# Adaptive-norm transformer block: set-up with shift and scale from products on all partitions, h of the second batch among the rotations, turns between the runs, and means times powers by GpSimd

## The chip, the cores and the metric

The kernel runs on 1 core of one Trainium2 chip. The metric is the device time of the whole program in microseconds (us). TensorE (PE) multiplies matrices, VectorE (DVE) works elementwise and reduces, ScalarE (ACT) applies functions and scaled copies, GpSimd (POOL) works elementwise on SBUF, SyncE (SP) issues DMAs. DMAs are issued from the queues of SP, ScalarE and GpSimd.

## The reference

Everything is float32. x is 16 batches of 1024 rows by 256 columns; c is 16 x 256; wmod is 256 x 1536; there are 16 heads of 16 columns.

```python
mod = (silu(c) @ wmod).reshape(16, 6, 1, 256)
sa, ca, ga, sb, cb, gb = (mod[:, i] for i in range(6))
ga = sign(ga) * max(|ga|, 0.25)            # gb the same; sign(0) = 1
h = layernorm(x) * (1 + ca) + sa
x = x + ga * attention_block(h)            # h + Wo(softmax(rope(q) rope(k)^T / 4, causal) v) + bo,
                                           # q, k, v from layernorm(h) * ln_gamma + ln_beta
h = layernorm(x) * (1 + cb) + sb
x = x + gb * ffn(h)                        # 8 experts of 512 gathered rows each, scatter-add
```

So each batch needs two normalizations in a row ("x" and "h" in the names of the code): the first is scaled and shifted by that batch's rows of the modulation, and the second one's result is turned (transposed) for the products q, k and v. The modulation itself comes first of all: it is a product of all of c with wmod.

## The kernel before

The rows of a batch are two halves of 512 rows, a half four tiles of 128. The heads go in four groups of 4 (`G`). For each batch and group a pass of ten steps goes over the blocks of the causal triangle; steps 1 and 5 are *pair steps*, which take two narrow blocks at once (256 and 128 columns). A step does, for 4 heads: the scores of its block (L682, tile `s`), exp on ScalarE (L695, tile `p`), a select on GpSimd on diagonal blocks (L700), and the products with the values (L729, tile `o`), one step later. At the same time it works out the row maxima of the next pass: a product (L605, tile `m`) and a reduction on VectorE (L623, or L627 with the mask). Scores and maxima are issued in two bursts of four products, called runs in the title: `burst(0)`, then one other product (`first`), then `burst(1)`, then the `second`. All of these use six PSUM slots (`ps_s`, tag `s`), so a burst can begin only when the reductions and exps of products before it have freed slots.

Other work of the batch ahead is placed into these steps by hand: the turns (`step_xT`, L485, evacuated by ScalarE at L486 into `xnT`), q and k (`step_qk`, L510) with the rotations on VectorE (L517, tile `rot`) and their sums on GpSimd (`step_rot`, L533 and L534), written to DRAM and read back by head (`operands`), v (`step_v`, L541), the output projection (L821). `pieces` are TensorE's pieces, `extra` comes after a step, and `inside` is popped by VectorE one item after each reduction of a step (`between`), the rest by `drain()`.

`steps_h(b, half)` makes the two normalizations of one half: statistics (L387, L392) on VectorE, the power -0.5 on GpSimd (L397, L398, tile `rstd`), minus mean times power on VectorE (`less_mean`, L406, tile `nmr`), the normalization on ScalarE (L415), scale and shift with the rows of the modulation (`turn`, L428, on GpSimd; on VectorE for the first half of batch 0), and then for the residual `rest` (L438: bias bo and gate) and `onto` (L442). `H_AT` says at which group and step each of these stands for batches 2 and up. For batch 1 `spread` places them, and for batch 0 they are issued in the set-up.

The set-up, before the loop: loads; `modulation(half)`, which multiplies (L259), copies (L266), adds 1 and bounds the gates on 16 partitions (L268 to L275) and writes the result to DRAM (`mod_a` for the first half), from where `load_mod(b)` reads the three rows of a batch onto all partitions; the tables of the angles (`tables`, L290 to L297); batch 0's normalizations, turns, q, k and rotations; the maxima of the first pass (`own(n)`, ten units); v; batch 1's first half; `indices()`, which loads the experts' indices (L313) and transposes them (L318).

In the attention's end, `finish(c)` copies the sums of half c, sends the denominators through DRAM, takes the reciprocal on VectorE (L789, waits for the DMA `den`) and sends it back as `rec`; later GpSimd multiplies (L797). `to_do` puts the reciprocal inside step +2 and the multiplication after step +5 (half 0) or +4 (half 1):

```python
            inside[step + 2].append(first)
            extra[step + (4 if c else 5)].extend(others)
```

The order on TensorE, VectorE, ScalarE and GpSimd is that of the program; in the set-up that of SP too. What is computed after the attention (the experts) is not touched.

Of the kernel before, what the change touches and what calls it, by code (L numbers as in the profile page):

```python
# [19 lines left out]
P = 128  # L20
# [7 lines left out]
def adaln_block_kernel(  # L28
# [50 lines left out]
    mhalf = const.tile([P, NT], F32, name="mhalf")  # L79
    nc.vector.memset(mhalf, -0.5)  # L80
# [115 lines left out]
    with ExitStack() as actx:  # L196
# [54 lines left out]
        def modulation(half):  # L251
# [3 lines left out]
            m3 = mod[:B, o : o + 3 * D]  # L255
            for n in range(2):
                ps = ps_s.tile([P, QC], F32, name=f"pmod{half}_{n}", tag="s")
                for k in range(KC):
                    nc.tensor.matmul(  # L259
                        ps[:B, :w],  # L260
                        lhsT=sg[:, k, :],
                        rhs=wm[k][:, o + n * w : o + (n + 1) * w],
                        start=(k == 0),
                        stop=(k == KC - 1),
                    )
                nc.scalar.copy(m3[:, n * w : (n + 1) * w], ps[:B, :w])  # L266
# [32 lines left out]
        def output_bias():  # L299

            pbo = ps_1.tile([P, D], F32, name="pbo", tag="misc")
# [8 lines left out]
            nc.vector.tensor_tensor(bo_bc, pbo, bo_bc, ALU.add)  # L310

        def indices():
            nc.sync.dma_start(out=idx, in_=top_idx.rearrange("(t p) e -> p t e", p=P))  # L313
# [22 lines left out]
        def constants():  # L336
# [21 lines left out]
            for t in v_tiles:  # L358
                nc.gpsimd.memset(t, 0.0)
                nc.vector.memset(t[:, :, 0 : H * VW + 1 : VW], 1.0)  # L360
            for t in rec:
                nc.gpsimd.memset(t, 0.0)
            nc.vector.tensor_reduce(
# [11 lines left out]
        def steps_h(b, half, named=False):  # L375
# [5 lines left out]
            passes = nc.vector if (b, half) == (0, 0) else nc.gpsimd  # L381

            def stat(of, i):
                if i == 0:
                    mine["st"] = wk.tile([P, TC, 6], F32, name=f"st_{of}_{b}_{half}", tag="st")
                src = s["x"][:, half * TC + i, :] if of == "x" else s["h", half][:, i, :]
# [8 lines left out]
            def power(of):  # L395
                mine["r"] = wk.tile([P, TC], F32, name=f"rstd_{of}_{b}_{half}", tag="rstd")
                nc.gpsimd.tensor_tensor(mine["r"], mine["mv"][:, :, 1], eps[:, :TC], ALU.add)  # L397
                nc.gpsimd.tensor_tensor(mine["r"], mine["r"], mhalf[:, :TC], ALU.pow)  # L398

# [4 lines left out]
            def less_mean(of):  # L404
                mine["n"] = wk.tile([P, TC], F32, name=f"nmr_{of}_{b}_{half}", tag="nmr")
                nc.vector.scalar_tensor_tensor(mine["n"], mine["mean"], -1.0, mine["r"], ALU.mult, ALU.mult)  # L406

            def norm(of, u):
                if of == "x" and u == 0:
                    s["h", half] = lk.tile([P, TC, D], F32, name=f"h_{b}_{half}", tag="h")  # L410
                if u == 0 and not named:
                    less_mean(of)
                h = s["h", half]
                for i in (2 * u, 2 * u + 1):
                    nc.scalar.activation(  # L415
                        h[:, i, :],
                        s["x"][:, half * TC + i, :] if of == "x" else h[:, i, :],
# [8 lines left out]
            def turn(u, n, op):  # L426
                h = s["h", half][:, ts(u, 2), :]
                passes.tensor_tensor(h, h, row(n), op)  # L428

            def rest(u, n, op):  # L430
                if n is None and u == 0 and b > 0:
                    mine["rest"] = lk.tile([P, TC, D], F32, name=f"r_{b}_{half}", tag="r", bufs=1)
                elif n is None and u == 0:
                    if half == 0:
                        s["rest"] = big_tile([P, NT, D], "r_0")
                    mine["rest"] = s["rest"][:, ts(half, TC), :]
                r = mine["rest"][:, ts(u, 2), :]
                (passes if n is None else nc.gpsimd).tensor_tensor(r, s["h", half][:, ts(u, 2), :] if n is None else r, row(n), op)  # L438
# [5 lines left out]
            if named:  # L444
                pieces = {f"{of}{i}": lambda of=of, i=i: stat(of, i) for of in "xh" for i in range(TC)}
                for of in "xh":
                    pieces[of + " moments"] = lambda of=of: moments(of)
                    pieces[of + " power"] = lambda of=of: power(of)
                    pieces[of + " less"] = lambda of=of: less_mean(of)
                for u in range(2):  # L450
                    pieces[f"x norm{u}"] = lambda u=u: norm("x", u)
                    pieces[f"scale{u}"] = lambda u=u: turn(u, 1, ALU.mult)
                    pieces[f"shift{u}"] = lambda u=u: turn(u, 0, ALU.add)
                    pieces[f"bias{u}"] = lambda u=u: rest(u, None, ALU.add)
                    pieces[f"h norm{u}"] = lambda u=u: norm("h", u)
                    pieces[f"gate{u}"] = lambda u=u: rest(u, 2, ALU.mult)
                    pieces[f"onto{u}"] = lambda u=u: onto(u)
                return pieces

            return (  # L460
                [("v", lambda i=i: stat("x", i)) for i in range(TC)]
                + [("g", lambda: whole("x"))]
                + [("v", lambda u=u: norm("x", u)) for u in range(2)]
                + [("g", lambda u=u: turn(u, 1, ALU.mult)) for u in range(2)]
                + [("g", lambda u=u: turn(u, 0, ALU.add)) for u in range(2)]
                + [("v", lambda i=i: stat("h", i)) for i in range(TC)]
                + [("g", lambda: whole("h"))]
                + [("g", lambda u=u: rest(u, None, ALU.add)) for u in range(2)]
                + [("v", lambda u=u: norm("h", u)) for u in range(2)]
                + [("g", lambda u=u: rest(u, 2, ALU.mult)) for u in range(2)]  # L470
                + [("g", lambda u=u: onto(u)) for u in range(2)]
            )
# [388 lines left out]


        def spread(items, first, last):

            n = 0
            for at in range(first, last):
                want = -(-len(items) * (at - first + 1) // (last - first - 3))
                count = {"v": 0, "g": 0}
# [503 lines left out]
```

## Time and profile before

| what | before |
|---|---|
| runs | 2884.34, 2889.95, 2890.49 us, median 2889.95 |
| profiled execution | 2886.74 us, its span 2885.0 us |
| busy, share of the span: PE, DVE, ACT, POOL | 97%, 74%, 57%, 54% |
| first rotation (L517) | at 45.74 us |
| first reduction of the maxima (L627) | at 62.17 us |
| first scores (L682) | at 99.12 us |
| mean granted TensorE clock | 0.986 |

The page gives times from the start of the span. A row of the timeline has the start, the length, engine, line, operation and tiles, then in brackets the idle time of that engine before it and what ended it. A busy TensorE is not TensorE at its peak: matmuls overlap and their ends are modelled, so a stall inside a burst shows only in where the next matmul starts.

### The profile page before, as it was taken

Reading aid. Unit: us, or ns where it says so; the run is one execution under the profiler, and the core shown is the slowest. Engines: PE = TensorE matmul, PEld = TensorE weight load, DVE = VectorE, ACT = ScalarE, POOL = GpSimd, SP = SyncE. Lnnn points to the kernel's source line nnn. Section 1 sums busy time; section 2 is a strip of 40 time slices with the busy share of each in tenths; the row PEclk is TensorE's granted clock in tenths of the full one; section 3 lists DMA queues with packets and bytes.
Section 4 is the critical chain, followed back from the end, with each engine's and each line's share of the span. In section 5 each row is a group of like instructions: output and inputs, shape, how many; then the busy total and the mean of one; then the engine's idle time right before and its main releaser. Section 6 shows DMA issues by size and latency. Waiting matters only on the chain.

```text
span 2885.0 us, 62886 instructions
## 1 busy us (share of the span) xinstructions
PE 2810.8 (97%) x22373; PEld 1289.4 (45%) x22373; DVE 2125.2 (74%) x6810; ACT 1651.1 (57%) x3342; POOL 1562.6 (54%) x2063
## 2 busy tenths in 40 slices
PE   5899999999999999999999999999999999997998
PEld 3444444444444444444444444444444444443665
DVE  5777878777787878787877878787878777763554
ACT  2356666666666566666666666656666655653111
POOL 5455464546555555546454655555464666354553
PEclk7899999999999999999999999999999999998999
DMA  4211121222222222212222222222121212134552
GB/s 122 58 44 35 50 71 52 64 56 68 59 56 56 64 61 63 60 51 66 63 59 62 64 54 58 60 67 62 50 71 51 75 41 65 32 95 153 176 184 67
DMA packets 200154, 199.58 MB, mean 69 GB/s; under 512 B 93344, under 2 KB 154208, under 8 KB 199840
## 3 DMA queue, kind: packets, MB, share of 16 engines
q1 hardware_dynamic: 172240, 147.69, 18.9%
q0 software_dynamic: 8448, 24.78, 2.7%
q10 hardware_dynamic: 19152, 23.08, 2.6%
q8 instruction: 177, 2.90, 0.4%
q14 instruction: 137, 1.12, 0.1%
HBM read 118.67 MB, written 75.66 MB: 67 GB/s over the span
## 4 chain that ended last, share of the span: by engine, by line
PE 90%; DMA 3%; DVE 2%; POOL 2%; issue 1%; ACT 1%; SPq 0%; POOLq 0%; DVEq 0%; ACTq 0%
PE s L682 39%; PE o L729 20%; PE pqk L510 9%; PE m L605 7%; PE pw L821 4%; PE pv L541 4%; PE fo L1229 2%; PE ph L1204 2%; PE ptx L485 1%; DMA out_dram<-fy,idx 1%; DMA cur<-out_dram,idx 1%; POOL modg L98 1%; ACT p L695 0%; DMA ops<-rot 0%; DVE nmr_h L406 0%
## 5 line engine op out<-in xcount | busy, mean ns | idle before, releaser
L695 ACT ACTIVATE p<-s 128x512 f32<-128x512 f32 (+1 forms) x2560 | 1278.9, 552 | 895.5 <-PE m L605 797.4
L605 PE MATMUL m<-ko,qo 32*128 32x512 f32 (+3 forms) x6144 | 1439.5, 527 | 7.0 <-DVE mt L623 4.7
L682 PE MATMUL s<-qo,ko 32*128 32x512 f32 (+3 forms) x6144 | 1359.1, 526 | 0.6 <-DMA qo<-max 0.5
L700 POOL TENSOR_SCALAR_AFFINE_SELECT p<-p 128x256 f32<-128x256 f32 x1024 | 416.1, 414 | 1002.4 <-ACT p L695 1001.2
L623 DVE TENSOR_REDUCE mt<-m 128x1 f32<-128x512 f32 x1024 | 673.0, 683 | 203.9 <-PE m L605 184.2
L682 PEld LDWEIGHTS s<-qo,ko 32*128 32x128 f32 x6144 | 514.8, 183 | 597.3 <-issue 423.6
L729 PE MATMUL o<-p,v_pad 128*32 128x512 f32 (+3 forms) x6840 | 652.7, 464 | 3.2 <-POOL p L700 2.8
L627 DVE CUSTOM_DVE_ANT_0 masked<-m,dmask,mt 128x256 f32<-128x256 f32 (+3 forms) x1024 | 511.4, 539 | 142.6 <-PE m L605 132.1
L627 DVE CUSTOM_DVE_ANT_0 masked<-m,dmask 128x512 f32<-128x512 f32 (+3 forms) x1024 | 453.9, 485 | 189.3 <-PE m L605 170.2
L605 PEld LDWEIGHTS m<-ko,qo 32*128 32x128 f32 x6144 | 576.6, 184 | 30.2 <-DVE mt L627 11.2
L729 PEld LDWEIGHTS o<-p,v_pad 128*32 128x32 f32 x6840 | 149.0, 108 | 427.8 <-issue 180.0
L510 PE MATMUL pqk<-xnT,wqk 128*128 128x256 f32 x1024 | 287.3, 405 | 1.8 <-ACT xnT L486 1.3
L510 PEld LDWEIGHTS pqk<-xnT,wqk 128*128 128x128 f32 x1024 | 175.3, 190 | 193.0 <-issue 148.5
L428 POOL TENSOR_TENSOR h<-h,mod 128x512 f32<-128x512 f32 x124 | 157.6, 1274 | 76.5 <-ACT h L415 70.9
L627 DVE DVE_READ_ACCUMULATOR2_ANT mt<- 128x1 f32 x2048 | 168.7, 82 | 0.0
L541 PE MATMUL pv<-wv_sb,xnT 128*128 128x256 f32 x512 | 146.9, 410 | 1.1 <-ACT xnT L486 0.9
L821 PE MATMUL pw<-wo,onT 128*128 128x256 f32 x512 | 144.2, 405 | 0.6 <-DVE onT L778 0.6
L1207 ACT ACTIVATE gT<-ph,b_sb 128x512 f32<-128x512 f32 x64 | 44.0, 687 | 174.1 <-PE ph L1204 169.1
L541 PEld LDWEIGHTS pv<-wv_sb,xnT 128*128 128x128 f32 x512 | 87.9, 191 | 98.5 <-issue 76.5
L517 DVE SCALAR_TENSOR_TENSOR rot<-pqk,bcol,cosT 128x256 f32<-128x256 f32 x256 | 122.0, 477 | 11.6 <-PE pqk L510 8.3
L821 PEld LDWEIGHTS pw<-wo,onT 128*128 128x128 f32 x512 | 86.9, 189 | 89.3 <-issue 70.9
L517 DVE SCALAR_TENSOR_TENSOR rot<-pqk,bcol,sinT 128x256 f32<-128x256 f32 x256 | 121.3, 474 | 0.6 <-DMA ops<-rot 0.6
(122 smaller groups left out, 2239.5 us busy)
## 6 DMA issues: line engine op xcount, KB each, us to landing
ops<-rot SPq DMA_DIRECT2D x128, 256.0 KB
rec<-rec_d SPq DMA_DIRECT2D x504, 32.0 KB
rows<-y SPq DMA_DIRECT2D x62, 256.0 KB
out_dram<-y SPq DMA_DIRECT2D x62, 256.0 KB
w<-in_W_dram SPq DMA_DIRECT2D x14, 1024.0 KB
qo<-ops SPq DMA_DIRECT2D x192, 64.0 KB
ko<-ops SPq DMA_DIRECT2D x192, 64.0 KB
x<-in_x_dram ACTq DMA_DIRECT2D x24, 512.0 KB
```

The costliest lines, as they stand in the source:

```text
L428: passes.tensor_tensor(h, h, row(n), op)
L510: nc.tensor.matmul(ps, lhsT=wqk[:, k, n, e, :], rhs=xt[:, k, ts(u, QW)], start=(k == 0), stop=(k == KC - 1))
L517: nc.vector.scalar_tensor_tensor(s["rot", half, n, e, f][:, ts(u, QW)], ps, bcol[:, n, e : e + 1], tab[:, half * QC + u * QW : half * QC + ...
L541: nc.tensor.matmul(pv, lhsT=S[b]["xnT", t // TC][:, k, ts(t % TC, P)], rhs=wv_sb[:, k, :], start=(k == 0), stop=(k == KC - 1),)
L605: nc.tensor.matmul(sc[:, sum(w[:n]) : sum(w[: n + 1])], lhsT=q[rows, ts(i, P)], rhs=k[rows, c * QC : c * QC + w[n]], start=True, stop=True,)
L623: nc.vector.tensor_reduce(dst, sc[:, 0:w], AX.X, ALU.max, negate=True)
L627: nc.vector.tensor_tensor_reduce(out=masked[:, 0:w], in0=sc[:, 0:w], in1=dmask[:, QC - w : QC], scale=-1.0, scalar=mt[half][:, 0, h, i % T ...
L682: nc.tensor.matmul(sc[:, o:e], lhsT=k[rows, ts(j_, P)], rhs=q[rows, c_ * QC + q0 : (c_ + 1) * QC], start=True, stop=True,)
L695: nc.scalar.activation(p[:, h, 0:end], sc[:, 0:end], AF.Exp, scale=scale)
L700: nc.gpsimd.affine_select(out=mine, in_=mine, compare_op=ALU.is_ge, fill=0.0, base=0, pattern=[[0, 3 - n], [0, n], [1, P]], channel_multip ...
L729: nc.tensor.matmul(acc[c][W * g : W * (g + 1), q0:q1], lhsT=v[:, j, h * VW + 1 - DH * (G % 2) : h * VW + 1 - DH * (G % 2) + W], rhs=p[:, g ...
L821: nc.tensor.matmul(po, lhsT=s["onT", c][:, k, ts(t, P)], rhs=s["wo"][:, k, :], start=(k == 0), stop=(k == KC - 1),)
```

## The change

It has four parts.

*Set-up.* The angle tables are loaded first on ScalarE's queue, then Wq and Wk; all small loads, Wo and bv, and also batch 1's x, the second half of wmod, Wv and the indices, go to SP's queue, behind the first loads. `tables()` runs ahead of the normalizations. `first_rows()` multiplies batch 0's column of silu(c), broadcast to 128 columns, with the shift and scale parts of wmod, so that both rows stand on all partitions in PSUM (`pm`). Batch 0's scale and shift are then done by VectorE from PSUM: `(1 + m) * h`, and `h + m` into the tile for the residual. The products of the modulation, their copies and the VectorE work on them are three separate pieces; the last comes after the first turns. Batch 1's first half has its statistics, normalization, scale and shift between batch 0's rotations; its rest, batch 0's bias, gate and sum, all of v, both its turns and the indices stand among the units of the first maxima. Batch 1's second half is placed by a list (`H_FIRST`) in place of `spread`.

*Means times powers.* `less_mean` on VectorE goes; `power` gains two GpSimd products (mean times power, times -1).

*Turns between the runs.* In a pair step that has a turn, the turn comes between the two bursts and the values' product after the second one; it was the other way round.

*The reciprocal of half 0* goes from inside step +2 (a pair step) to the end of step +3; the statistics that stood in those steps move by one to three steps.

```diff
+        def first_rows():
+            pm = ps_1.tile([P, 2, D], F32, name="pm0", tag="acc")
+            for k in range(KC):
+                nc.tensor.matmul(
+                    pm.rearrange("p a d -> p (a d)"),
+                    lhsT=sg[:, k, 0:1].to_broadcast([P, P]),
+                    rhs=wm[k][:, 0 : 2 * D],
...
         def indices():
-            nc.sync.dma_start(out=idx, in_=top_idx.rearrange("(t p) e -> p t e", p=P))
...
+            shifted = lambda: s["rest"][:, ts(half, TC), :] if b == 0 else s["h", half]
...
+                mine["n"] = wk.tile([P, TC], F32, name=f"nmr_{of}_{b}_{half}", tag="nmr")
+                nc.gpsimd.tensor_tensor(mine["n"], mine["mean"], mine["r"], ALU.mult)
+                nc.gpsimd.tensor_tensor(mine["n"], mine["n"], minus[:, :TC], ALU.mult)
...
-            def less_mean(of):
-                mine["n"] = wk.tile([P, TC], F32, name=f"nmr_{of}_{b}_{half}", tag="nmr")
-                nc.vector.scalar_tensor_tensor(mine["n"], mine["mean"], -1.0, mine["r"], ALU.mult, ALU.mult)
...
-                passes.tensor_tensor(h, h, row(n), op)
+                if b > 0:
+                    nc.gpsimd.tensor_tensor(h, h, row(n), op)
+                    return
+                if (half, u, n) == (0, 0, 1):
+                    s["rest"] = big_tile([P, NT, D], "r_0")
+                m = s["pm"][:, n : n + 1, :].to_broadcast([P, 2, D])
+                if n == 1:
+                    nc.vector.scalar_tensor_tensor(h, m, 1.0, h, ALU.add, op)
+                else:
+                    nc.vector.tensor_tensor(shifted()[:, ts(u, 2), :], h, m, op)
...
-            "x0 0 3, x1 0 4, x2 0 6, x3 0 8, x moments 0 9, x power 1 0, x less 1 3, x norm0 1 3, x norm1 1 4, "
+            "x0 0 3, x1 0 4, x2 0 8, x3 0 9, x moments 0 9, x power 1 0, x norm0 1 3, x norm1 1 4, "
...
+            for half in range(NC):
+                h_of(half, "x0", "x1", "x2", "x3", "x moments", "x power")
+            copies = modulation_products(0)
...
+            h_of(0, "x norm0", "x norm1")
+            h_of(1, "x norm0", "x norm1")
+            do(copies)
+            copies = modulation_products(1)
+            h_of(0, "scale0", "scale1", "shift0", "shift1", "h0", "h1", "h2", "h3", "h moments", "h power")
+            do(copies)
+            h_of(1, "scale0", "scale1")
+            h_of(1, "shift0", "shift1", "h0", "h1", "h2", "h3", "h moments", "h power")
+            h_of(0, "h norm0", "h norm1")
             do(turns[0])
+            modulation(0)
+            load_mod(0)
             load_mod(1)
+            h_of(1, "h norm0", "h norm1")
+            ones()
+            do(turned[0][:4] + rots[0][:1])
+            h_of(2, "x0", "x1", "x2", "x3", "x moments", "x power")
+            do(turned[0][4:])
+            do(turns[1])
+            h_of(2, "x norm0", "x norm1")
+            do(rots[0][1:])
+            operands(0, 0, 0)
+            h_of(2, "scale0", "scale1", "shift0")
+            do(turned[1][:4] + rots[1][:1])
+            h_of(2, "shift1")
+            do(turned[1][4:] + rots[1][1:])
+            operands(0, 0, 1)
+            joins = output_bias()
+            h_of(2, "h0", "h1", "h2", "h3", "h moments", "h power")
+            joins()
...
-            for n in range(mid):
+            for n in range(NS):
                 own(n)
+                do(vs[n - 1 : n] if n else [])
+                if n == 0:
+                    operands(0, 1)
+                    h_of(2, "bias0", "bias1", "h norm0", "h norm1")
+                if n == 1:
+                    modulation(1)
                 if n == mid:
                     place(0)
+                    indices()
+                if n == mid + 2:
+                    do(prep[1][0][0])
+                if n == mid + 3:
+                    h_of(2, "gate0", "gate1", "onto0", "onto1")
+                    for half in range(NC):
+                        h_of(half, "bias0", "bias1", "gate0", "gate1", "onto0", "onto1")
...
-            inside[step + 2].append(first)
+            inside[step + (2 if c else 3)].extend([first] if c else [nothing] * (GH - 1) + [first])
...
-                    elif mine and units and len(last) == 2:
+                    elif mine and units and 2 in (len(last), len(parts)):
                         first, second = mine, [lambda: product(last)]
```

## The prediction, made before the changed kernel ran

> **What bounds the kernel now.** I read the page first (the slices), then busy time by stage, the set-up's timeline, and last the groups and waits of what the change moves.
>
> ```profile
> span 2885.0 us, 62886 instructions
> PE   5899999999999999999999999999999999997998
> PEclk7899999999999999999999999999999999998999
> ```
> TensorE is full in all but the first and the last slices, so time is to be had at the start, in stalls too short for a slice, and at the end, which this change leaves alone. By stage (length, then busy time of PE, PEld, DVE, ACT, POOL, then clock, DMA share, GB/s):
>
> ```profile
> 0.00:45.74 45.74, 13.50 (x41) 7.97 (x42) 22.06 (x65) 13.34 (x25) 22.66 (x31) 0.70 0.42 129
> 45.74:62.17 16.43, 15.54 (x73) 12.77 (x73) 13.66 (x32) 2.10 (x4) 7.49 (x7) 1.00 0.31 82
> 62.17:99.12 36.95, 32.89 (x125) 14.90 (x123) 29.91 (x97) 6.49 (x15) 24.09 (x22) 0.86 0.26 68
> 99.12:114.48 15.36, 12.33 (x50) 6.46 (x49) 7.79 (x31) 6.55 (x12) 4.66 (x7) 0.56 0.41 114
> 426.00:584.00 158.00, 158.00 (x1336) 69.05 (x1332) 123.04 (x405) 100.04 (x205) 86.86 (x118) 1.00 0.23 60
> ```
> Before the first rotation (45.74) no engine is half busy: a chain of waits. Then VectorE leads (13.66 of 16.43, 29.91 of 36.95). The first loop steps run at clock 0.56. One batch of the loop then takes 158.0 us with TensorE busy throughout. The set-up's chain, from the timeline (start, length, idle before and its releaser):
>
> ```profile
> 18.25 0.84 ACT L266 COPY mod<-pmod 16x384 f32<-16x384 f32 x2 [13.87 <-DMA bo_bc<-in_bo_dram]
> 23.24 4.04 ACT L415 ACTIVATE h<-x,nmr_x,rstd_x 128x256 f32<-128x256 f32 x8 [4.15 <-DVE nmr_x L406]
> 27.50 5.38 POOL L428 TENSOR_TENSOR h<-h,mod 128x512 f32<-128x512 f32 x4 [2.23 <-DMA mod<-mod_a]
> 30.08 4.55 DVE L428 TENSOR_TENSOR h<-h,mod 128x512 f32<-128x512 f32 x4
> 40.16 2.08 ACT L415 ACTIVATE h<-h,nmr_h,rstd_h 128x256 f32<-128x256 f32 x4 [10.74 <-DVE nmr_h L406]
> 45.74 0.48 DVE L517 SCALAR_TENSOR_TENSOR rot<-pqk,bcol,cosT 128x256 f32<-128x256 f32 x1 [2.52 <-PE pqk L510]
> 106.56 0.37 PE L318 MATMUL ptok<-ident,idxf 128*32 128x128 f32 x1 [1.73 <-DVE idxf L316]
> 107.37 1.09 PE L485 MATMUL ptx<-ident,h 128*128 128x128 f32 x4 [0.43 <-ACT tok L320]
> 109.33 2.07 PE L541 MATMUL pv<-wv_sb,xnT 128*128 128x256 f32 x4 [0.87 <-ACT xnT L486]
> ```
> ScalarE issues DMAs until 18.2 us; only then is the modulation copied, worked over by VectorE, written, read back (27.5), applied, normalized again (40.16), turned and multiplied (45.74). Last, the stalls in the loop, by operation and by wait:
>
> ```profile
> L406 DVE SCALAR_TENSOR_TENSOR nmr_x<-mv_x,rstd_x x32: 149/156/349, 23.0 to 2288.3; 128x4 f32<-128x4 f32 x32
> L406 DVE SCALAR_TENSOR_TENSOR nmr_h<-mv_h,rstd_h x32: 150/600/3710, 38.8 to 2331.6; 128x4 f32<-128x4 f32 x32
> DVE inv L789 <- DMA den<-den_d: 34.4, 26, 6.1
> 2333.81 1.12 PE L682 MATMUL s<-qo,ko 32*128 32x512 f32 x2
> 2335.93 1.01 PE L605 MATMUL m<-ko,qo 32*128 32x512 f32 x1 [1.00 <-DVE mt L623]
> ```
> A 4-column product takes 150 ns on VectorE when nothing disturbs it, 600 at the median and 3710 at worst; behind the worst one TensorE's burst of eight, begun at 2333.81, is broken. The reciprocal L789 waits for its DMA 26 times.
>
> **Part 1, up to the first rotation.** The new order: angle tables first on ScalarE's queue, everything after the four weight loads on SP's; the first batch's shift and scale come from a product on all 128 partitions, left in PSUM, and VectorE applies them from there. Gone from the path: ScalarE's 13.87 us, the chain L268 to L275, the write and read-back of mod_a. In their place, from rows: SP issues x as before, and its statistics began at 8.84; 1.40 for four L387 and 0.36 for L392 give 10.6; the powers 1.32 (10.60 to 11.92) and two more GpSimd steps of 0.20 (row L397), 12.4; four L415, 2.07, 14.5. The tables (L290 to L297, 24.6 to 29.4 before) go ahead of this, while x is still coming. The four PSUM turns: the nearest low row is L438 on VectorE, 0.68, the high one L428 on VectorE, 1.18 mean while GpSimd was also adding. GpSimd adds nothing then, so I take 0.7: 2.8, from 13.6, ends 16.8; statistics 1.75 and powers 1.8 give 20.5. From the second L415 to L517 it was 5.6 us (40.16 to 45.74): 26.1.
>
> One new wait stands in that chain: ScalarE must copy the second half's modulation products before the second L415, and they need the second half of wmod, queued on SP behind x of batch 1 and seven small loads. 1.8 MB go out from about 11; the first 20 us moved 149 GB/s (nearest low price, 12 us) while x and the first wmod half, 1.8 MB, had come in about 8.5 (high): 20 to 23. Products at the pitch of L259 (4.08 for eight) and a copy push the second L415 to 24 to 27. Queued behind the waiting copies on ScalarE are the L415 on the path, and behind them all of TensorE. First rotation 26 to 33; I take 29.2: **-16.5** (-13 to -20).
>
> The Trainium skill's page "SBUF — State Buffer", section "SBUF: two separate sides", says that a VectorE instruction with two SBUF inputs and a GpSimd one take a port pair from each other for a whole instruction; an operand in PSUM would then escape it. The trace agrees: L428 on VectorE ran 677 to 1745 ns beside GpSimd, and the 3.71 us product ended with GpSimd's adds. By the rule the turns stay at the low row even beside GpSimd; by the high row the path is 2 us longer.
>
> **Part 2, first rotation to first scores** (53.4 us before: 45.74 to 99.12). VectorE's list: 32 rotations at a pitch of 0.43, 13.8; new between them, batch 1's statistics, two times 1.75, and a wait of about 2 for GpSimd, which now has eight rotation adds and four turns (12 x 1.27 = 15.2) in one queue; the bias 0.4: own maxima begin 20.5 after the first rotation (16.4 before). They cost VectorE 6.6 (62.17 to 68.8) and, row by row, 4 groups of 2.46, 2.7, 2.7 and 2.2, together 24.0; then modulation(1) 4.25 (71.65 to 75.9, again beside GpSimd) and 1 for transposes and indices. The moments, GpSimd turns and nmr stalls of batch 1 have left this stretch. GpSimd's 20 us of bias, gate and sum stand in the open there and end before the first select (20.5 + 2.5 + 20 = 43). With 2 us of residual waits, less the 2.7 by which the scores start before the last reduction: 20.5 + 29.3 + 2 - 2.7 = 49. I take 50: **-3.5** (0 to -7). The values' products add 1.1 each on TensorE, under reductions of 2.46.
>
> **Part 3, the first loop steps.** From 99.12 to 114.48, 15.4 us. The index load's wait, its transpose, the turns and a values product move into the set-up. What stays is two bursts (2.1), one short burst (0.9) and the values (1.0) at full clock: 4; at half clock 8. I take 6: **-9.5** (-7 to -11), and **-1** for the other values product. Batch 1's other half stays in the loop at new places: its two L415 now share a step (2.07 us on ScalarE, as in the 127.5 us step before), nil.
>
> The page "TensorE: Matmul & The Clock Gate", section "What's actually happening", has the clock halved after an idle window of some 3.4 us: it speaks against a set-up with gaps. The trace shows 0.56 here, after gaps no longer than 2.26 us since 62.17 (before 76.56), so the start may be cold again whatever the rule; that is the 8.
>
> **Part 4, the loop.** *Means times powers:* one VectorE product becomes two GpSimd ones of 0.20; 8 x 0.2 = 1.6 per batch on 86.86 of 158, hidden, though the selects queue behind them by 0.4. VectorE loses 0.15 to 0.6 four times a batch, and the 3.7 us stall near 2331 goes: **-4** (0 to -5). *The reciprocal of the first 512 rows* moves from a pair step to the end of the next. Where it waited (0.9 at 530) TensorE's next burst was late; elsewhere it frees 0.25 in a step where slots for the scores are short. Bound below by nil, above by the whole wait of 34.4 / 14 = 2.5 per batch, of which the larger part belongs to the second half's reciprocal, which stays: 0.8 per batch, over 14 batches **-11** (0 to -22). Late next: the multiplication on GpSimd, two steps (8 us) on instead of three; the other half has that distance already. *Turns between the runs:* after them the next burst was late by 0.2 to 0.3; now the second run of the pair step has the short gap instead, and the next the long one: nil (-1 to +1 per batch; in the range).
>
> **Sum.** -16.5 - 3.5 - 9.5 - 1 - 4 - 11 = -45.5. The profiled execution took 2886.74 (span 2885.0 and 1.74 around it): 2841.2. The median of the runs, 2889.95, is 3.2 above it: **2844**.
>
> **Rivals.** *Held by the loads:* the wmod half lands after 27 and SP's sixteen Wo and bv issues delay the gate rows: 10 us of part 1 remain lost, 2854. For it: ScalarE spent 13.87 us in such a queue; against: SP has little else before 30. *The loop keeps its 158 us:* stalls only change places; parts 1 to 3 alone, -30.5: 2859. For it: TensorE is shown busy all the time. Both together: 2869. *Slower:* the later reciprocal makes GpSimd wait for rec at the multiplication, selects queue behind, the values' products wait. Over 63 such passes it decides from 0.7 us a pass; GpSimd's longest wait for rec is 3.3 us, and at 1.2 a pass (+76, -34 for the rest) the time is 2932. Against it: 13 waits, 15 us in all, at the same distance now. I exclude that the change does nothing, since the set-up's chain has no parallel path.
>
> **How the numbers follow.** Forecast 0.60; held by the loads 0.15; unchanged loop 0.15; slower 0.08; nothing measurable 0.02. A measurement can tell 0.2%, about 6 us, from no change. Range 2822 to 2870: the low end takes parts 1 to 4 near their best (-68), the high end both rivals. Faster 0.90, same 0.02, slower 0.08.
>
> **What would show it.** The first L517 near 29, the first scores near 79, no index transpose after them; no L406 on VectorE, one reciprocal wait a batch left; 157 us a batch or less. I am wrong if the first rotation stays beyond 36, or if a batch takes more than 158 with GpSimd waiting for rec.

## The result, and the profile after

| | before | after |
|---|---|---|
| median of four runs beside each other | 2887.14 us | 2854.12 us (2849.76 to 2859.05) |
| after / before | | 0.9882, interval 0.986 to 0.9904 |
| profiled execution, span | 2886.74, 2885.0 us | 2856.21, 2854.5 us |
| first rotation (L517, now L528) | 45.74 us | 29.14 us |
| first own reduction (L627, now L638) | 62.17 us | 49.99 us |
| first scores (L682, now L693) | 99.12 us | 86.28 us |
| batch 0, first scores to the second batch's | 172.55 us | 165.18 us |
| batches 2 to 14, mean of 13 periods | 157.45 us | 156.86 us |
| fifteenth period | 163.48 us | 158.42 us |
| the sixteenth batch and the experts | 403.0 us | 405.4 us |

The kernel became 33 us faster, 1.2% by the ratio; the forecast was 2844, the range 2822 to 2870. The spans differ by 30.5, and the rows of the table say where: -16.6 to the first rotation, +3.8 from there to the first scores, -7.4 in batch 0, -7.7 in thirteen batches, -5.1 in the fifteenth, +2.4 at the end, which the change leaves alone (over the profiled executions of all the kernels below, the end varies between 397.5 and 405.7).

The page, TensorE's slices:

```profile
PE   6999999999999999999999999999999999997998
```
The slices hardly show the change: half of it lies inside the first digit. The stages show it (length, then busy time of PE, PEld, DVE, ACT, POOL, clock, DMA share, GB/s), cut at the same events as before, with the loop's window at the end:

```profile
0.00:29.14 29.14, 16.30 (x49) 8.49 (x50) 23.24 (x64) 14.40 (x27) 16.24 (x33) 0.93 0.57 177
29.14:49.99 20.85, 18.90 (x84) 15.06 (x83) 16.83 (x49) 4.17 (x8) 15.20 (x16) 0.93 0.46 127
49.99:86.28 36.29, 27.53 (x125) 14.44 (x125) 31.54 (x83) 7.38 (x16) 25.31 (x23) 0.81 0.21 57
86.28:94.39 8.11, 8.11 (x41) 5.01 (x41) 7.17 (x28) 4.02 (x7) 1.62 (x4) 0.73 0.25 58
426.00:584.00 158.00, 157.76 (x1345) 68.57 (x1341) 123.82 (x405) 100.95 (x207) 88.58 (x126) 1.00 0.23 60
```
Up to the first rotation VectorE is now busy 23.24 of 29.14 us, where it was 22.06 of 45.74: the waits went, the work stayed. The third row is the surprise: from the own maxima to the scores it takes 36.29 us, nearly the old 36.95, though work had left this stretch, and VectorE is busy in 31.54 of it. In the loop TensorE's busy time tells nothing: 157.76 of 158 in a kernel whose batch is 0.6 us shorter.

The set-up's chain in the timeline (start, length, idle before and its releaser; x2 is a sum over two), to be read against the chain of before:

```profile
4.70 3.77 POOL L379 MEMSET v_pad<- 128x2184 f32 x2
4.73 5.28 DVE L311 COPY wide<-tab 128x512 f32<-128x512 f32 x2
12.15 1.40 DVE L410 BATCH_NORM_STATS2 st_x<-x 128x6 f32<-128x256 f32 x4
17.07 0.69 DVE L455 SCALAR_TENSOR_TENSOR h<-pm,h 128x512 f32<-128x512 f32 x1 [1.29 <-ACT h L435]
...
21.71 0.47 ACT L281 COPY mod<-pmod 16x384 f32<-16x384 f32 x1 [0.63 <-PE pmod L274]
23.55 2.07 ACT L435 ACTIVATE h<-r,nmr_h,rstd_h 128x256 f32<-128x256 f32 x4 [1.38 <-POOL nmr_h L424]
29.14 0.48 DVE L528 SCALAR_TENSOR_TENSOR rot<-pqk,bcol,cosT 128x256 f32<-128x256 f32 x1 [1.28 <-PE pqk L521]
25.58 0.27 DVE L291 TENSOR_SCALAR sign<-mod 16x256 f32<-16x256 f32 x1
55.49 1.34 DVE L291 TENSOR_SCALAR sign<-mod 16x256 f32<-16x256 f32 x1
57.93 2.71 POOL L469 TENSOR_TENSOR x<-x,r 128x512 f32<-128x512 f32 x2
66.94 1.30 DVE L335 TENSOR_SCALAR widx<-idx 128x32 int32<-128x32 int32 x1
69.61 0.37 PE L338 MATMUL ptok<-ident,idxf 128*32 128x128 f32 x1 [2.33 <-DVE idxf L336]
```
The shift and scale are applied from PSUM at 17.07, the second normalization runs at 23.55 (40.16 before), and the waits left in the chain are about 1.3 us each. Two things stand in these rows that were not costed. The table copies, 5.28 for two, lie beside GpSimd's memsets and put the statistics off to 12.15. Taken one by one, the first copy lasts 4.95 us, from 4.73 to 9.69, and the second 0.41; GpSimd works off four memsets in that time (1.91, 1.91, 0.51 and 0.51 us, the last ending at 9.40), so the copy was held through all four and not through one. And one and the same operation of L291 on 16 partitions takes 0.27 at 25.58 and 1.34 at 55.49, where GpSimd adds without a break (2.71 for two).

The waits between 110 and 2600 us, total, times, longest:

```profile
DVE inv L800 <- DMA den<-den_d: 35.0, 20, 6.2
POOL part L808 <- DMA rec<-rec_d: 17.8, 22, 3.1
POOL onT L808 <- DMA rec<-rec_d: 14.2, 7, 5.0
```
The reciprocal's waits are 20 instead of 26 but no shorter in sum. In the loop proper (270 to 2290) it is 23.3 us in 16, where it was 19.9 in 19. Sorted by half, all 16 are half 1's, which the change does not move, and 22.5 us of it are one wait a batch, in the fourth pass. Half 0's were 3.2 us in four before and are gone, and half 1's grew from 16.8. GpSimd's waits for `rec` at the multiplication rose from 15.0 us in 13 before to 32.0 in 29, by 0.3 a pass, against the 0.7 from which the rival "slower" would decide.

### The profile page after: what moved, and what is told of

It is laid out like the page before. It is cut to its first block, busy times and chain, and to the rows that moved or that the text cites. A ratio compares the mean times of both kernels' runs of the same rounds, so it can differ in the third digit from the quotient of the medians.

```text
span 2854.5 us, 63015 instructions
## 1 busy us (share of the span) xinstructions
PE 2793.4 (98%) x22385; PEld 1279.2 (45%) x22385; DVE 2119.8 (74%) x6749; ACT 1650.7 (58%) x3342; POOL 1579.7 (55%) x2189
## 4 chain that ended last, share of the span: by engine, by line
PE 93%; DVE 3%; issue 1%; POOL 1%; ACT 1%; DMA 1%; another core or an unknown queue 0%; POOLq 0%; SPq 0%; ACTq 0%; DVEq 0%
PE s L693 40%; PE o L740 21%; PE pqk L521 9%; PE m L616 5%; PE pv L552 5%; PE pw L832 5%; PE ph L1232 4%; PE fo L1257 3%; PE ptx L496 1%; DVE mt L634 1%; DVE rot L528 0%; PE fpt L1221 0%; ACT p L706 0%; ACT h L435 0%
## 5 line engine op out<-in xcount | busy, mean ns | idle before, releaser
L616 PE MATMUL m<-ko,qo 32*128 32x512 f32 (+3 forms) x6144 | 1417.1, 527 | 6.2 <-DVE mt L638 3.7
L693 PE MATMUL s<-qo,ko 32*128 32x512 f32 (+3 forms) x6144 | 1370.2, 526 | 0.8 <-ACT h L435 0.7
L693 PEld LDWEIGHTS s<-qo,ko 32*128 32x128 f32 x6144 | 523.4, 183 | 597.3 <-issue 365.8
L740 PE MATMUL o<-p,v_pad 128*32 128x256 f32 (+3 forms) x6848 | 651.8, 464 | 2.8 <-POOL p L711 2.5
L638 DVE CUSTOM_DVE_ANT_0 masked<-m,dmask,mt 128x256 f32<-128x256 f32 (+3 forms) x1024 | 515.6, 547 | 123.5 <-PE m L616 121.9
L638 DVE CUSTOM_DVE_ANT_0 masked<-m,dmask 128x512 f32<-128x512 f32 (+3 forms) x1024 | 454.0, 485 | 187.9 <-PE m L616 162.3
L616 PEld LDWEIGHTS m<-ko,qo 32*128 32x128 f32 x6144 | 561.6, 184 | 21.9 <-DVE mt L638 13.3
L638 DVE DVE_READ_ACCUMULATOR2_ANT mt<- 128x1 f32 x2048 | 170.2, 83 | 0.0
L528 DVE SCALAR_TENSOR_TENSOR rot<-pqk,bcol,cosT 128x256 f32<-128x256 f32 x256 | 122.0, 477 | 7.6 <-PE pqk L521 7.1
L528 DVE SCALAR_TENSOR_TENSOR rot<-pqk,bcol,sinT 128x256 f32<-128x256 f32 x256 | 121.7, 475 | 0.9 <-DMA ops<-rot 0.9
```

Source lines behind the costliest of these rows:

```text
L528: nc.vector.scalar_tensor_tensor(s["rot", half, n, e, f][:, ts(u, QW)], ps, bcol[:, n, e : e + 1], tab[:, half * QC + u * QW : half * QC + ...
L616: nc.tensor.matmul(sc[:, sum(w[:n]) : sum(w[: n + 1])], lhsT=q[rows, ts(i, P)], rhs=k[rows, c * QC : c * QC + w[n]], start=True, stop=True,)
L638: nc.vector.tensor_tensor_reduce(out=masked[:, 0:w], in0=sc[:, 0:w], in1=dmask[:, QC - w : QC], scale=-1.0, scalar=mt[half][:, 0, h, i % T ...
L693: nc.tensor.matmul(sc[:, o:e], lhsT=k[rows, ts(j_, P)], rhs=q[rows, c_ * QC + q0 : (c_ + 1) * QC], start=True, stop=True,)
L740: nc.tensor.matmul(acc[c][W * g : W * (g + 1), q0:q1], lhsT=v[:, j, h * VW + 1 - DH * (G % 2) : h * VW + 1 - DH * (G % 2) + W], rhs=p[:, g ...
```

## The experiments

All ratios are to the kernel before on the same chip and carry a 95% interval. "Period" is the mean of the same 13 batches, from the profiled execution.

**The changed kernel once more**, as the base of what follows.

> The changed kernel again, beside the others on their chip. Forecast's theory for the kernel with the old order of the turns, which was 10 us faster than the changed kernel had been: its loop is not shorter (156.85 against 156.86 us a batch); it had no half-clock stretch between 77 and 2590 us, the changed kernel's profile had two of 6.8 us (at 90.0 and 137.8), so the changed kernel's times should spread over 2844 to 2856 as such stretches come and go. Rival: the order of the turns costs 6 us or more in the first batch each time; then all runs lie at 2849 or above.

Measured: 2849.42 against 2885.55, ratio 0.988 (0.9864 to 0.9897); first rotation 28.99, first scores 85.97, batch 0 159.85, period 156.98, fifteenth 156.23. The milestones repeat to 0.3 us, but batch 0 is 5.3 us shorter in the same program. The clock says why; first a window of batch 0 in the profiled execution of the table, then the same window in this run (columns as in the stages):

```profile
120.00:150.00 30.00, 28.40 (x220) 12.69 (x216) 21.00 (x75) 15.68 (x32) 18.61 (x28) 0.89 0.19 52
```
```profile
120.00:150.00 30.00, 28.25 (x245) 13.15 (x240) 22.46 (x77) 19.28 (x40) 20.27 (x30) 1.00 0.20 48
```
The mean clock is 0.89 against 1.00: the first profile had two stretches of 6.8 us at half clock in batch 0 (from 90.0 and from 137.8), the second none. So single milestones of batch 0 are good to about 5 us only, and its -7.4 is -12.7 in the second profile. The profiles of the other new versions below fit. Batch 0 takes 159.5 to 161.0 us in the five of them all with no half-clock stretch in it, 163.0 and 163.6 in the two with one of 6.8 us, and 165.2 to 165.8 in the three with two; in the three with one of 3.4 us it takes 160.7 to 162.7.

The third stage does not follow the clock: from the first own reduction (48.66) to the first scores this run takes 37.31 us at a mean clock of 0.68, the first profile 36.29 at 0.81.

**The reciprocal back in the pair step.**

```diff
-            inside[step + (2 if c else 3)].extend([first] if c else [nothing] * (GH - 1) + [first])
+            inside[step + 2].append(first)
```


> The changed kernel with one part undone: the reciprocal of half 0 is back inside step +2 (its multiplication and the moved statistics stay as changed). My forecast's theory: it was the main gain in the loop; the mean batch period of batches 2 to 14 goes from 156.9 us back by 0.4 to 157.3, the time from 2854 to about 2860. Rival (stalls only change places): period within 0.1, time 2853 to 2856.

Measured: 2854.68 against 2883.13, 0.9902 (0.9886 to 0.9919). The period is 157.51, within 0.06 of the 157.45 before: with the rest of the change in place, the reciprocal's new place is worth 0.53 to 0.65 a batch, as much as the whole gain. Over seven profiles in which nothing in the loop differs from the changed kernel (the two of it and five of the versions below that move work in the set-up alone), the period is 156.86 to 157.17, so this is 0.34 outside their spread. The total does not separate it from the changed kernel.

**The turns back behind the values' product.**

```diff
-                    elif mine and units and 2 in (len(last), len(parts)):
+                    elif mine and units and len(last) == 2:
```


> The changed kernel with one part undone: in pair steps with a turn, the values' product comes between the two bursts again and the turn after them. Forecast's theory: nil, the late burst only moves from after the turn to before it; period 156.9 within 0.1, time 2852 to 2857. Rival: the order of the turns is what shortened the loop; period 157.3 or more, time 2860 or more.

Measured: 2844.08, 0.9867 (0.9851 to 0.9884); period 156.85; the fifteenth period starts at 2286.23, in the changed kernel's second profile at 2286.51. The turns' order is worth nothing in the loop. The total is 39.1 below the kernel before, that of the second profile's runs 36.1, and the intervals of the two ratios overlap. In the profiles the difference lies behind the loop: the sixteenth batch starts at 2443.14 here and 2442.74 there, and the rest takes 400.8 against 403.8 us.

**The means times powers back on VectorE.**

```diff
-                nc.gpsimd.tensor_tensor(mine["n"], mine["mean"], mine["r"], ALU.mult)
-                nc.gpsimd.tensor_tensor(mine["n"], mine["n"], minus[:, :TC], ALU.mult)
...
+                nc.vector.scalar_tensor_tensor(mine["n"], mine["mean"], -1.0, mine["r"], ALU.mult, ALU.mult)
```


> The changed kernel with one part undone: minus mean times power is on VectorE again, at the places of the kernel before. Forecast's theory: the long product near the fifteenth batch comes back and costs 4 to 5 us there, the other batches lose 0.1 each; time about 2860. Rival (two more GpSimd products in front of the selects cost as much as VectorE gains): the fifteenth batch is 4 us longer but the others 0.2 shorter, time 2855 or less.

Measured: 2857.04, 0.9915 (0.9899 to 0.9932). First rotation 31.18, so 2 us later; period 156.78, unchanged; fifteenth 161.03 against 158.42 and 156.23. This product cost nothing in an ordinary batch, 2.6 to 4.8 us in the fifteenth and 2 in the set-up; in the totals against the kernel before it is 7 to 10.

**All three back** (the three edits above together). What stays new is the set-up with the list for batch 1's second half and, in every batch of the loop, the places of the statistics, one to four steps off the old ones.

> The changed kernel with all three loop parts undone, so the set-up alone is new. If the parts add up: batch periods as before (157.4), the fifteenth batch 163, time 2854 + 13 = 2867, that is 20 below the kernel before. Rival: the parts overlap or hinder each other, so this is under 2862 or over 2872.

Measured: 2858.53, 0.992 (0.9903 to 0.9936): 24.6 us faster without the three parts, 8 to 12 less than with them. First scores 88.86, period 157.09, fifteenth 161.46. The fifteenth is back as it was with the product alone. The period misses the expectation: with all three undone the loop should have gone back to 157.5, and it lies within the spread of the changed loop (156.86 to 157.17). So the reciprocal's 0.6 a batch depends on what stands around it, and what takes it up here stays open. The waits for `den` in the loop proper don't settle it: 21.8 us here, 29.2 with the reciprocal alone put back, 19.9 in the kernel before. The moved statistics are the one part of these batches that no run undoes, so the gain of 0.6 a batch may be theirs as well.

**Modulation of batch 1 and the index arithmetic ahead of the rotations**, before GpSimd's queue opens: the same instructions, earlier.

```diff
             load_mod(1)
+            modulation(1)
             h_of(1, "h norm0", "h norm1")
             ones()
+            nc.vector.tensor_single_scalar(bidx, idx, shift, ALU.arith_shift_right)
+            nc.vector.tensor_scalar_min(widx, idx, float(N - 1))
+            nc.vector.tensor_copy(idxf, idx)
...
-                if n == 1:
-                    modulation(1)
```


> The changed kernel with the second half's work on the modulation, and the three index operations of VectorE, moved in front of the first rotation, where GpSimd has nothing long to do. Theory (GpSimd's open queue of adds stands against VectorE's work on SBUF: seven operations of 1.24 to 1.37 us and two of 1.30, 10 us in all, against 0.25 to 0.41 each for the first half): the operations take under 3 us in all, first rotation at 30 to 31 us, first scores at 76 to 79 instead of 86.3, time 6 to 9 less. Rival (TensorE at half clock or the operands of the second half bound this stretch): first scores at 83 or later.

Measured: 2842.82 against 2849.42 for the changed kernel beside it, 0.9851 (0.9835 to 0.9868); the ranges of the two do not touch. First scores 77.42, 8.6 earlier, though the first rotation is 1.0 later. Its timeline:

```profile
27.52 0.27 DVE L291 TENSOR_SCALAR sign<-mod 16x256 f32<-16x256 f32 x1
29.79 0.16 DVE L983 TENSOR_SCALAR widx<-idx 128x32 int32<-128x32 int32 x1
```
0.27 and 0.16, where the same two rows of the changed kernel are 1.34 and 1.30. That is the missing time of the third stage: from the first own reduction to the first scores it is 28.34 us now, where it was 36.29, at the same mean clock (0.82 and 0.81), so that this run's rival is out. (The operations on the modulation are six, not seven, and the first took 0.91.)

**GpSimd's memsets out of the table copies' way**, to behind the norms.

```diff
-            for t in v_tiles:
-                nc.gpsimd.memset(t, 0.0)
-            for t in rec:
-                nc.gpsimd.memset(t, 0.0)
...
             h_of(1, "h norm0", "h norm1")
-            ones()
+            zeros()
...
             do(turned[0][4:])
+            ones()
```


> The changed kernel with GpSimd's zeroing of the v and rec tiles moved from 4.7 us to behind the powers of batch 0 (and the ones in the v tiles behind the first half's rotations). Theory (the table copies on VectorE, 5.28 us for two where a later one takes 0.43, wait for GpSimd's memsets): the copies are done by 6.5, the first statistics start at about 9 instead of 12.15, the first rotation at 26 instead of 29.1, time about 3 less. Rival (the copies wait for the load of the angle tables): nothing moves, first rotation at 29.

Measured: 2849.02, 0.9874 (0.9857 to 0.989), the changed kernel's time. Its timeline:

```profile
4.73 0.74 DVE L311 COPY wide<-tab 128x512 f32<-128x512 f32 x2
10.17 1.41 DVE L412 BATCH_NORM_STATS2 st_x<-x 128x6 f32<-128x256 f32 x4 [2.49 <-DMA x<-in_x_dram]
19.82 5.04 PE L274 MATMUL pmod<-wm,sg 128*16 128x384 f32 x8 [5.48 <-DMA wm<-in_wmod_dram]
22.58 0.47 ACT L281 COPY mod<-pmod 16x384 f32<-16x384 f32 x1 [3.41 <-PE pmod L274]
```
Half of the expectation holds: the copies take 0.74 instead of 5.28, and the statistics start 2 us earlier, now waiting for x. The gain is lost at the next wait: ScalarE waits 3.41 us for the products of wmod's second half, TensorE waits 5.48 for that half's load and then takes 5.04 for the eight products (2.75 for the first half's), and the first rotation comes at 30.7. So the memsets cost nothing while the loads set the pace, and this is where "held by the loads" is true.

**Shift and scale through the rows in DRAM again**, the rest of the set-up as changed (the rotations, the loop, the order of the loads but for Wo, bv and bo).

```diff
-            first_rows()
...
-                if n == 1:
-                    nc.vector.scalar_tensor_tensor(h, m, 1.0, h, ALU.add, op)
-                else:
-                    nc.vector.tensor_tensor(shifted()[:, ts(u, 2), :], h, m, op)
+                nc.vector.tensor_tensor(h if n == 1 else shifted()[:, ts(u, 2), :], h, row(n), op)
...
             do(copies)
+            modulation(0)
+            load_mod(0)
+            load_mod(1)
```


> The changed kernel with batch 0's shift and scale read back from DRAM as before (no product on all partitions): the first half's modulation is worked over by VectorE, written and read back ahead of the scaling, and SP's loads of Wo, bv and bo stand behind that. Theory (the rows in PSUM are worth the chain of VectorE, the write and the read-back, 2.4 + 6.3 us, and the freed ScalarE queue the rest of the 16.6): first rotation at 37 to 40, time 8 to 11 more than the changed kernel. Rival (the freed queue is the gain): first rotation at 33 or earlier, time 4 or less more.

Measured: 2865.29 against 2892.69, 0.9903 (0.9887 to 0.992). Its timeline:

```profile
28.38 1.29 DVE L453 TENSOR_TENSOR h<-h,mod 128x512 f32<-128x512 f32 x2 [5.62 <-DMA mod<-mod_a]
```
VectorE waits 5.62 for the row to come back, and the first rotation is at 40.80. Of part 1's 16.6 us the product on all partitions is thus 11.7; the order of the loads and the rest are 5. In the totals this kernel keeps 27.4 us of a gain of 33 to 36, so the totals show 6 to 9 of the 11.7.

**Both halves' reciprocals a step later.**

```diff
-            inside[step + (2 if c else 3)].extend([first] if c else [nothing] * (GH - 1) + [first])
-            extra[step + (4 if c else 5)].extend(others)
+            inside[step + 3].extend([nothing] * (GH - 1) + [first])
+            extra[step + 5].extend(others)
```


> The changed kernel, with the reciprocal of half 1 also moved to the end of step +3 and its multiplication to step +5. Theory (the wait that is left is the one by half 1 in the fourth pass, one burst late by 1.45 us a batch there): period 156.9 goes to 155.5 to 156.3, time 8 to 18 us less, about 2842. Rival (TensorE makes up for it elsewhere, or the multiplication then waits for rec and delays the selects): period 156.7 or more, time 2851 or more.

Measured: 2854.72 against 2849.42 for the changed kernel, 0.9899 (0.9881 to 0.9917); period 157.86 against 156.98. The ranges of the runs overlap (2851.18 to 2860.24, and 2848.21 to 2852.45). Its waits between 110 and 2600:

```profile
POOL part L808 <- DMA rec<-rec_d: 79.9, 44, 4.8
DVE inv L800 <- DMA den<-den_d: 6.2, 1, 6.2
```
VectorE's wait is gone (35.0 to 6.2), and GpSimd's at the first multiplication has taken its place (17.8 to 79.9). This is the mechanism of the rival "slower", at the other half.

**Three versions to beat the changed kernel.** The first joins the two set-up moves above and puts the second half of wmod before batch 1's x.

```diff
-            load_x(1)
             load_wm(1)
+            load_x(1)
```

> The changed kernel with three moves: the second half's modulation work and the index operations ahead of the first rotation; GpSimd's zeroing behind the powers; and on SP's queue the second half of wmod ahead of batch 1's x. Theory (with the zeroing moved, the first rotation was held at 30.7 by ScalarE waiting 3.41 and 1.85 us for products that wait for the second wmod half): this wait goes, first rotation at 26 to 28, first scores at 73 to 76, time 8 to 11 less than the changed kernel. Rival (TensorE at half clock holds the products): first rotation at 30 or later, first scores at 77 or later.

Measured: 2846.27 against 2892.69, 0.9841 (0.9824 to 0.9857). First scores 76.56, but the first rotation is at 30.44, not 26 to 28. ScalarE's copies are early now (16.93), so the loads are no longer late. The timeline shows what is:

```profile
24.86 3.87 DVE L292 TENSOR_SCALAR sign<-sign 16x256 f32<-16x256 f32 x1
24.83 3.77 POOL L378 MEMSET v_pad<- 128x2184 f32 x2
```
The two moves collide: two memsets of 1.9 us start at 24.83, and L292 of `modulation(1)`, 0.28 us elsewhere, lasts until both are done. The rotation has no idle time before it; it queues behind that on VectorE. TensorE, too, runs at clock 0.57 between 20 and 28 us, so that how much either of the two holds is open.

The second puts the loads of batch 0's x before the first wmod half.

```diff
-            load_wm(0)
             load_x(0)
+            load_wm(0)
```

> The kernel with three moves and a fourth: batch 0's x is loaded ahead of the first half of wmod. Theory (with the zeroing moved VectorE waits for x until 10.17 and 12.57): statistics start at about 8, first rotation 1 to 2 us earlier than with three moves. Rival (the products with wmod, then the later one, hold the path): same within 0.5 us.

Measured: 2847.68, 0.9846 (0.983 to 0.9863), the same time: the statistics come earlier, and the same memsets (from 23.89) hold the same L292 (23.93, 3.87 us).

The third moves half 1's reciprocal a step later as well, but only in the last pass, where it had waited for its DMA.

```diff
-            inside[step + (2 if c else 3)].extend([first] if c else [nothing] * (GH - 1) + [first])
-            extra[step + (4 if c else 5)].extend(others)
+            late_c1 = c and step % (NG * NS) == (NG - 1) * NS
+            inside[step + (2 if c and not late_c1 else 3)].extend(
+                [first] if c and not late_c1 else [nothing] * (GH - 1) + [first]
+            )
+            extra[step + (4 if c and not late_c1 else 5)].extend(others)
```


> The kernel with four moves and a fifth: of half 1 only the reciprocal that falls into the fourth pass of a batch goes to the end of step +3, its multiplication to step +5. Theory (this one waits 2.3 us for its DMA each batch and makes one burst 1.45 us late, while moving all of them made GpSimd wait for rec, 83 us in place of 34): period 0.6 to 1.3 us a batch shorter, time 8 to 16 less than with four moves. Rival (GpSimd's wait for rec takes it back): period within 0.3.

Measured: 2829.55 (2827.58 to 2833.61), 0.9784 (0.9768 to 0.9801): 18 us below the second version beside it, 63 below the kernel before, and faster than both kernels of this case. Period 156.12. Its waits:

```profile
DVE inv L799 <- DMA den<-den_d: 9.5, 8, 6.2
```
In the second version this was 38.9. Here VectorE's wait goes and nothing on GpSimd replaces it (its wait at the first multiplication is 17.3, in the second version 17.0; at the other, `onT`, 2.2 and 14.5): the difference to the move of every such reciprocal is which passes are moved.

## Why the prediction was right, and where not

*Part 1* (forecast -16.5 to a first rotation at 29.2; measured -16.6, 29.14). The sum is right, its items less so, and that it came out to 0.1 us is luck. The table copies were put beside the x load at no cost and lasted 5.28 us, so that the statistics came at 12.15 instead of 8.84. The wait for wmod's second half, which the forecast put at a second normalization of 24 to 27, did not bind: ScalarE's copies were done at 22.18 (21.71 and 0.47), and the second normalization, at 23.55, waited for `nmr_h` from the late statistics. Two errors cancelled. When the first is mended alone, the wait is there and the time is unchanged. The price of a turn from PSUM, 0.7, was right (0.69). The product on all partitions carries 11.7 of it.

*Part 2* (forecast -3.5; measured +3.8). This is the term that failed, by 7.3, and with it the sign that was named for it, first scores near 79 (86.28). Nearly all of it lies behind the start of the own maxima: 20.85 us up to them was costed at 20.5 (the items named add up to 19.7), the rest at 29.5 and took 36.29. The step that failed is "modulation(1) 4.25 ... and 1 for transposes and indices": GpSimd's 20 us "in the open" were counted as time that GpSimd has, not as time that VectorE loses beside it. Modulation took 7.46 us and the indices 2.9, with GpSimd busy in every part of both, and TensorE waited 2.33 for the indices; VectorE then waited 2.55 and 2.06 for TensorE's maxima, where the sum had 2 for all waits. The price of 4.25 came from a chain of which only half lay beside GpSimd. In the kernel before, two of its six operations stand in these rows, with the adds that the first one met:

```profile
71.96 2.59 POOL L442 TENSOR_TENSOR x<-x,r 128x512 f32<-128x512 f32 x2
72.08 1.34 DVE L270 TENSOR_SCALAR sign<-mod 16x256 f32<-16x256 f32 x1
74.73 0.41 DVE L273 TENSOR_TENSOR mag<-mod,sign 16x256 f32<-16x256 f32 x1
```
The three operations that met these adds took 0.50, 1.34 and 1.24, the three behind them 0.41, 0.28 and 0.41. In the changed kernel all six lie beside adds and take 0.91 to 1.37 each. The same instructions ahead of that queue bring the first scores 8.6 us forward.

That is also where the Trainium skill's page "SBUF — State Buffer", section "SBUF: two separate sides", had more to say than the prediction took from it. Beside instructions with two SBUF inputs it names VectorE's two-port modes as what shares a lock with GpSimd. The rows fit: copies with one input, 0.74 us for two, took 5.28 beside the memsets, and 0.28 became 3.87; that these instructions run in such a mode, no run here shows. The prediction drew on the rule only for the PSUM turns; it should have been asked of the small instructions beside GpSimd's queue. And the "whole instruction" that the prediction took from it is too little: the copy was held through four of GpSimd's.

*Part 3* (forecast -9.5 and -1; measured -7.4 in the first profile, -12.7 in the second). First scores to the second short burst took 8.1 us instead of 15.4, by the table of stages, against a forecast of 6: half clock, which the prediction had as its high end, came in one execution and not in the other. In that other one the same stretch, 85.97 to 92.50, took 6.5 us at a mean clock of 1.00, so the term itself was sized right. The stretch at half clock from 90.0 came with no idle time of TensorE above 0.9 us in the 13 us before it, so that the idle window cited in the prediction did not decide it.

*Part 4* (forecast -4, -11 and nil). The product's stall in the fifteenth: -5.1, and undoing it brings 2.6 to 4.8 back. The reciprocal was put at 0.8 a batch, and the loop gained 0.5 to 0.6, so -6 to -8 in thirteen batches; undoing the reciprocal alone gives the old period, undoing it with the other two parts doesn't, so that this gain is the reciprocal's is not shown. The larger wait was not removed but left at the other half, as the prediction said. The turns: nil.

*The rivals.* The total alone would not have told the forecast from them: 2854 is the very number of "held by the loads", and 5 below that of the unchanged loop. The milestones do. The loads did not hold this kernel's first rotation, at 29.14 where that rival had it 10 later, though they stand right behind what did. The loop did not keep its time, by 0.6 a batch. The mechanism of "slower" is real, and it decides by the pass, not by the half: for half 0 the later reciprocal left no wait of GpSimd for `rec` above 2.7 us in the loop proper (over the whole stretch the longest is 5.0, and it was 3.5 before, not 3.3); for half 1 in all passes the period grew by 0.9 and the median by 5 us; for half 1 in one pass of four it gained 18.

The total thus came out 10 above the forecast. The terms are 7.3 from part 2, 3.1 from part 3, 3.3 from the reciprocal and 2.4 at the end, less 1.1 from the fifteenth batch and 0.1 from part 1, in the spans, together 15 (-45.5 against -30.5); 5 of these are not seen in the medians: the forecast added 3.2 for a median above the profiled execution, and the changed kernel's median lay 2.1 below its profiled execution.

## What to carry to other kernels

When a helper engine's work is moved into the open, cost the other engine's small instructions beside it again: each may wait for one whole instruction of the helper, or for several in a row, so a row taken from a quiet stretch is too low, here by a factor of three to eight beside adds and of twelve and more beside memsets. Put chains of small VectorE instructions where GpSimd is between steps, not where it has a queue, and do not move a long memset in front of them either. A wait for a DMA should be moved pass by pass: look up which passes wait, and move only those, since the next consumer has the same few microseconds to lose.

## What the runs showed of the hardware

GpSimd memsets held a VectorE copy (4.95 us through four of them, instead of 0.40) and a 16-partition scalar operation (3.87 through two, instead of 0.28), although a memset has no input tile. Nor is one GpSimd instruction the most that can go ahead: the product of 3.71 us near 2331 in the kernel before began 0.02 behind an add of 1.27 and ended 0.03 behind the third in a row. Instructions on 16 partitions of 256 elements took 0.91 to 1.37 us beside GpSimd's adds (1.31 to 1.45 each), instead of 0.25 to 0.41, and index operations of 0.16 took 1.30. The same program had stretches of half TensorE clock at 90.0 and 137.8 in one execution and none there in another, worth 5 us in batch 0 (no idle time of TensorE above 0.9 us stands in the 13 us before either). And a TensorE that is shown busy for 158.00 us of the window from 426 to 584 in the kernel before, and for 157.76 in the changed kernel and in the last version, still gained 1.3 us a batch, from 157.45 to 156.12.
